# PSUM handed out in pairs of banks: one read for seven zones, for two heads' scores and for both row sums; maxima once per group; first loads in another order

## The chip, the cores and the metric

The kernel runs on one core of one Trainium2 chip, in float32. The metric is the device time of one execution in microseconds. The kernel before took 2783.18 us (median of 3 executions, 2778.69 to 2783.46). PE is TensorE, PEld its loading of weights, DVE VectorE, ACT ScalarE, POOL GpSimd, SP the engine that issues most of the transfers. PSUM holds what matmuls write: eight banks of 512 floats for each of 128 partitions.

## The reference

One layer of attention over graphs, with a layer norm before it. x is 128 graphs of 128 nodes by 768 features; adj is 128 x 128 for each graph; 12 heads of 64.

```python
h = jnp.maximum(_layernorm(x, axis=-1), 0.0)
q, k, v = (_split_heads(h @ W + b) for W, b in ((Wq, bq), (Wk, bk), (Wv, bv)))
scores = jnp.einsum('bhqd,bhkd->bhqk', q, k) / jnp.sqrt(HD)
scores = scores + beta * adj_e                       # adj_e = adj[:, None]
scores = jnp.where(adj_e > 0, scores, -9e15)
probs = jax.nn.softmax(scores, axis=-1)
out = x + merge_heads(jnp.einsum('bhqk,bhkd->bhqd', probs, v))
```

## The kernel before

The function `direct` does the work. It caps scores instead of subtracting their maximum; it keeps the largest row sums, reciprocals and biases that it sees in a small tile `seen`, and a second, general version would run if one of them passed a bound.

**Groups and slices.** The 128 graphs go in 32 groups of four, so that one matmul operand has 512 columns (4 graphs x 128 nodes). A group's projections are made in three slices: `qk0` (queries and keys of heads 0 to 5), `v`, and `qk1` (queries and keys of heads 6 to 11). Each slice multiplies a 2 x 3 by a 3 x 3 block matrix with 15 products in place of 18 (`PRODUCTS`), whose operands are sums of blocks: `SUMS_A` and `inner` make those of the activations (DVE at L411, POOL at L418 to L421), `SUMS_B` those of the weights. Products accumulate in four chains, a, b, c and d: the products of one chain add up in the same PSUM bank, and after each product the bank's running sum is read and added to, or subtracted from, the outputs that it belongs to.

**Two forms of a product.** Slices `qk0` and `v` of groups 1 to 31 use `product_z`, which splits a product once more, into seven zones of 128 columns (28 matmuls at L495). The prepared weights `T` of each product lie in DRAM and are loaded ahead by SP through a ring of five. A chain there holds two banks, zones 0 to 3 and 4 to 6. Slice `qk1` uses `product` (16 matmuls at L571 into one bank). After a product, the first read of an output ("opening") is made by ACT with the bias (L514 to L517 for qk0, L581 for qk1; in `v` half on DVE at L508 and L510), the others by DVE as an addition (L521 and L522 for the two banks of zones, L587 in qk1).

**Order.** `run` goes through the 15 slots of a slice. In a slot it issues the product's matmuls, then the steps written for that slot in `todo`, then the weighing of finished attention (`weighing`), then what is due from earlier slots (`later`), then the product's reads, then the "post" steps. From L981 to L1074 every engine's instructions stand in the order in which they are written; the start (group 0's first slice) and the last slice are ordered by a scheduler. The products of `product_z` come in the order `ZORDER`, chains by slot c, d, c, d, a, c, a, b, a, b, a, c, b, c, b. In qk1 the chains by slot are c, a, c, b, d, a, c, b, d, c, a, b, c, a, b.

**Attention.** `scores` makes the scores of two heads (one 128-feature block `oc`) for four graphs, one bank for each head (L609); DVE caps them and adds the bias (L613), ACT exponentiates (L616). `attend` gives eight steps of matmuls (L646) that `turn` puts one by one between the zones or columns of a slot's product; each of its two banks (r = 0 and 1) holds 4 x 65 columns, the 65th being the row sums. `weigh` bounds the sums (L623), takes reciprocals (L624), folds both into `seen` (L626), and then ACT divides, one activation for each graph and head (L630). POOL adds the block to x (L656), and SP stores it six slots later. In `qk0` of group G the attention of blocks 3 to 5 of group G-1 begins at slots `AV_Z`; in `qk1` that of blocks 0 to 2 of group G at slots `AV_AT`. The bias tile of the next group is made in `qk0` in steps (L436 to L449): a transpose, the mask, a masked copy on DVE (L444), a square on ACT (L445), a maximum into `seen`.

**Banks.** Eight bank tiles go round in a queue: `take` gives the one that has been free longest, `give` puts one back when its last reader has been issued.

```python
free = deque(psum.tile([P, W], F32, name=f"bank{i}") for i in range(8))
take, give = free.popleft, free.append
```

**Start.** Group 0 is made by `plain_slice` (L784) with unsplit products, beside the loading of the weights and the making of `T`; `raw_qk` and `raw_v` load the weights, `rows_1` and `rows_2` normalise the first x.

Of the kernel before, what the change touches and what calls it, by code (L numbers as in the profile page):

```python
# [17 lines left out]
P = 128  # L18
# [84 lines left out]
AV_Z = (7, 9, 12)  # L103
# [11 lines left out]
def direct(ctx, tc, x, adj, wq, bq, wk, bk, wv, bv, beta, out, bad):  # L115
# [31 lines left out]
    free = deque(psum.tile([P, W], F32, name=f"bank{i}") for i in range(8))  # L147
    take, give = free.popleft, free.append
# [31 lines left out]
    seen = const.tile([P, 20], F32, name="seen")  # L180

    over = const.tile([P, 44], F32, name="over")
# [19 lines left out]
    def raw_qk(u, t, parts):  # L202

        v = t.rearrange("p (c i j n) -> p c i j n", c=NC, i=2, j=3)
        for lo, hi in parts:
            for i, name in enumerate(("q", "k")):
                load_cols(nc.sync, v[:, :, i, lo:hi].rearrange("p c j n -> p c (j n)"), name, (lo + 3 * u) * P)
# [91 lines left out]
    raw_qk(0, flat(0, 9), ((0, 1),))  # L299
    load_x(0, 1)  # L300
    raw_qk(0, flat(0, 9), ((1, 3),))
# [131 lines left out]
    def bias_steps(G):  # L433
# [48 lines left out]
    def product_z(G, sl, n):  # L482
# [4 lines left out]
        if first:  # L487
            banks[chain] = (take(), take())
        p = [b.rearrange("p (z w) -> p z w", w=P) for b in banks[chain]]
        a, s, b = A[G, an], SP[G, n], tz.pop((G, sl, n))  # L490
        acts = (a[:, 0, 0:N], s[:, 1], s[:, 2], a[:, 1, 0:N], s[:, 3], a[:, 1, N:H2], s[:, 0])
        for z in range(7):
            lhs, rhs = (acts[z], b[:, z]) if sl == "v" else (b[:, z], acts[z])
            for q in range(0, P, HD):
                nc.tensor.matmul(p[z // 4][q:q + HD, z % 4, :], lhs[:, q:q + HD], rhs, start=(first and z % 4 == 0),  # L495
                                 stop=True, skip_group_check=True)
            turn()
        load_T()
        yield
        for (r, j), sign in uses:  # L500
            key = (G, sl, r, j)
            op = ALU.add if sign > 0 else ALU.subtract
            if key not in qk:
                left[key] = sum(k == (r, j) for q in PRODUCTS for k, _ in q[3])
                t = qk[key] = home_qk(*key, zones=True)
                if sl == "v":
                    bias = bv_b[:, j * 2 * P:(j + 1) * 2 * P]
                    added[G] = nc.vector.tensor_tensor(t[:, 0], bias[:, 0:P], p[0][:, 0], op)  # L508
                    nc.scalar.activation(t[:, 1:4], p[0][:, 1:4], AF.Copy, scale=float(sign))
                    added[G] = nc.vector.tensor_tensor(t[:, 6], bias[:, P:2 * P], p[1][:, 2], op)  # L510
                    nc.scalar.activation(t[:, 4:6], p[1][:, 0:2], AF.Copy, scale=float(sign))
                else:
                    oc = j + 3 * int(sl[2])
                    nc.scalar.activation(t[:, 0], p[0][:, 0], AF.Identity, bias=bqk[:, 0, oc:oc + 1], scale=float(sign))  # L514
                    nc.scalar.activation(t[:, 1:4], p[0][:, 1:4], AF.Copy, scale=float(sign))
                    nc.scalar.activation(t[:, 4:6], p[1][:, 0:2], AF.Copy, scale=float(sign))
                    opened[0] = nc.scalar.activation(t[:, 6], p[1][:, 2], AF.Identity, bias=bqk[:, 2, oc:oc + 1],  # L517
                                                     scale=float(sign))
            else:
                t = qk[key]  # L520
                nc.vector.tensor_tensor(t[:, 0:4], t[:, 0:4], p[0], op)  # L521
                added[G] = nc.vector.tensor_tensor(t[:, 4:7], t[:, 4:7], p[1][:, 0:3], op)  # L522
# [3 lines left out]
        if n == mine[-1]:  # L526
            for b in banks.pop(chain):
                give(b)
# [70 lines left out]
    def scores(G, u, order=(2, 0, 1)):  # L599

        order = [3 * u + j for j in order]
        ps = {(oc, i): take() for oc in order for i in range(2)}
        for oc in order:
            for g in range(GRP):
                keys, queries = (side(G, u, g // 2, oc % 3, i, g % 2) for i in (1, 0))
                for i in range(2):
                    r = slice(i * HD, (i + 1) * HD)
                    for k in range(0, N, HD):
                        nc.tensor.matmul(ps[oc, i][k:k + HD, g * N:(g + 1) * N], keys[r, k:k + HD], queries[r],  # L609
                                         start=True, stop=True)  # L610
# [7 lines left out]
    watched, recip = {}, {}  # L618

    def weigh(G, oc, r, pa, o):  # L620

        t = stat.tile([P, 2, 4], F32, tag="sm", name=f"sm_{G}_{oc}_{r}")
# [14 lines left out]
    def attend_steps(G, oc):  # L637
        o = work.tile([P, 2, 4, HD], F32, tag="o", name=f"o_{G}_{oc}", bufs=2)
        for r in range(2):
            bank = take()  # L640
            pa = bank[:, 0:4 * VE].rearrange("p (b e) -> p b e", e=VE)
            for g in range(2):
                for i in range(2):
# [5 lines left out]
                    if g == i == 1:  # L649
                        weighing.append(lambda r=r, pa=pa, bank=bank: (weigh(G, oc, r, pa, o[:, r])(), give(bank)))  # L650
# [14 lines left out]
    def scores_half(G, oc, r):  # L665
# [13 lines left out]
        e = es[G, oc, r] = work.tile([P, 2, 2, N], F32, tag="e", name=f"e_{G}_{oc}_{r}", bufs=6)  # L679
# [7 lines left out]
    def attend_half(G, oc, r):  # L687
# [15 lines left out]
        if not r:  # L703
            weigh(G, oc, r, pa, o)()
# [5 lines left out]
        at = 20 + 8 * (oc - 3)  # L710
        nc.vector.tensor_scalar(over[:, at:at + 4], pa[:, :, HD], SUM_CAP, None, op0=ALU.is_ge)
        nc.vector.tensor_scalar(over[:, at + 4:at + 8], pa[:, :, HD], 1.0 / SUM_CAP, None, op0=ALU.is_le)
        m = stat.tile([P, 2, 4], F32, tag="sm", name=f"sm_{G}_{oc}_{r}")
# [102 lines left out]

    turned[0, "raw"] = load_adj(0)
    nc.sync.dma_start(bv_b, bv[None, :].to_broadcast([P, D]))
    raw_v()
# [24 lines left out]
    def rows_2(g, mv, r):  # L844

        v = xg[0, g].rearrange("p b (c j) -> p c b j", c=NC)
        for k in range(3):
            n = work.tile([P, 2, P], F32, tag="e", name=f"rows_{g}_{k}", bufs=6)
# [149 lines left out]
    attention(0, 0, (11, 13, 15))  # L998
    for n in range(8):
        then(n, step, 2)  # L1000
# [87 lines left out]
    with tc.issue_after(watched[0].ins), tc.issue_after(recip[0].ins):  # L1088
        recip[0] = nc.vector.tensor_scalar(over[:, 0:20], seen, SUM_CAP, None, op0=ALU.is_ge)
# [4 lines left out]
    nc.tensor.matmul(pf[0:1, 0:44], ones, over, start=True, stop=True)  # L1094
    behind_recip(stores.pop(0), lambda: nc.vector.tensor_reduce(bad, pf[0:1, 0:44], AX.X, ALU.max))
# [129 lines left out]
```

## Time and profile before

| | |
|---|---|
| median of 3 executions | 2783.18 us (2778.69 to 2783.46) |
| the profiled execution | 2781.26 us, span 2779.2 us |
| TensorE clock granted over the span | 0.996 |
| PE busy | 2744.4 us, 99% |
| DVE, ACT, POOL busy | 2187.9 (79%), 1363.2 (49%), 2297.7 (83%) us |
| transfers | 660.87 MB, 238 GB/s over the span |

The time is that of the whole execution; the span is the part between the first and the last recorded instruction. A line of a group of instructions gives source line, engine, operation, output and inputs, shapes and count, then busy time in us, mean ns of one, and the idle time of the engine just before them with what ended it. A timeline line gives start and duration in us. A line of a stretch gives its length, then the busy time of PE, PEld, DVE, ACT and POOL with their counts, then the granted TensorE clock, the DMA share and GB/s.

### The profile page before, as it was taken

The numbers are of one execution on the slowest core, as the hardware profiler recorded it, in microseconds if no ns is written. First come the engines' busy times: TensorE is split into PE (matmuls) and PEld (weight loads), VectorE is DVE, ScalarE is ACT, GpSimd is POOL, SyncE is SP. The second block draws the span as 40 slices with busy tenths as digits, with TensorE's granted clock in tenths as the row PEclk, the third lists the DMA queues.
The fourth block names the chain that finished last, engine by engine and source line by source line (L and its number), as shares of the span: only waits on it lengthen the run. The fifth ranks groups of instructions, "written<-read, shape, count | busy, mean of one in ns | idle before, by whom it ended". The sixth has DMA issues, their size and how long they took to land.

```text
span 2779.2 us, 113442 instructions
## 1 busy us (share of the span) xinstructions
PE 2744.4 (99%) x46433; PEld 2401.3 (86%) x46433; DVE 2187.9 (79%) x4826; ACT 1363.2 (49%) x3999; POOL 2297.7 (83%) x4054
## 2 busy tenths in 40 slices
PE   8989999999999999999999999999999999999998
PEld 7678888899889998888989888988889989889887
DVE  5788878788878787787888787888787877878865
ACT  2445454555454554444554545554545544445543
POOL 3688988888988889888889888889888898888893
PEclk9999999999999999999999999999999999999999
DMA  8878878887878788778888788878787887788854
GB/s 212 232 239 235 237 236 236 267 251 230 239 228 258 253 249 237 234 232 264 255 238 233 233 239 268 255 228 242 226 261 253 249 234 237 231 265 253 232 185 129
DMA packets 526216, 660.87 MB, mean 238 GB/s; under 512 B 105460, under 2 KB 401664, under 8 KB 525696
## 3 DMA queue, kind: packets, MB, share of 16 engines
q1 hardware_dynamic: 525368, 653.20, 78.5%
q8 instruction: 368, 6.03, 0.9%
q14 instruction: 152, 1.25, 0.1%
q10 hardware_dynamic: 328, 0.40, 0.1%
HBM read 589.26 MB, written 64.21 MB: 235 GB/s over the span
## 4 chain that ended last, share of the span: by engine, by line


## 5 line engine op out<-in xcount | busy, mean ns | idle before, releaser
L630 ACT ACTIVATE o<-bank,sm 128x64 f32<-128x64 f32 x1524 | 354.7, 316 | 656.7 <-DVE sm L624 464.8
L495 PE MATMUL bank<-spbuf,T_qk 128*64 128x128 f32 x7440 | 660.6, 273 | 1.3 <-POOL spbuf L419 1.2
L495 PE MATMUL bank<-T_v,spbuf 128*64 128x128 f32 x7440 | 647.2, 273 | 0.1
L646 PEld LDWEIGHTS bank<-v,e 128*64 128x64 f32 x6048 | 419.3, 137 | 106.0 <-issue 0.8
L495 PEld LDWEIGHTS bank<-T_v,spbuf 128*64 128x64 f32 x7440 | 459.0, 137 | 0.4 <-ACT o L630 0.4
L495 PEld LDWEIGHTS bank<-spbuf,T_qk 128*64 128x64 f32 x7440 | 441.1, 137 | 2.1 <-POOL spbuf L419 1.4
L646 PE MATMUL bank<-v,e 128*64 128x65 f32 x6048 | 438.2, 221 | 0.2 <-ACT o L630 0.2
L495 PE MATMUL bank<-S,T_qk 128*64 128x128 f32 x4092 | 402.7, 274 | 2.5 <-DMA T_qk<-kept_qk 1.0
L495 PE MATMUL bank<-T_v,S 128*64 128x128 f32 x4092 | 402.0, 274 | 1.7 <-DVE v L521 0.7
L571 PE MATMUL bank<-S,wqk 128*64 128x256 f32 x2976 | 389.7, 380 | 0.0
L581 ACT ACTIVATE qk<-bank,bqk 128x256 f32<-128x256 f32 x372 | 156.6, 475 | 470.5 <-PE bank L571 362.2
L613 DVE SCALAR_TENSOR_TENSOR e<-bank,biasT 128x512 f32<-128x512 f32 x378 | 240.3, 685 | 90.4 <-PE bank L609 90.1
L571 PE MATMUL bank<-S,qk_T 128*64 128x256 f32 x2480 | 305.9, 379 | 0.0
L656 POOL TENSOR_TENSOR xo<-xo,o 128x512 f32<-128x512 f32 x189 | 242.4, 1283 | 50.0 <-ACT o L630 50.0
L551 POOL TENSOR_TENSOR v<-v 128x128 f32<-128x128 f32 x186 | 97.9, 526 | 224.5 <-DVE v L521 224.5
L495 PEld LDWEIGHTS bank<-T_v,S 128*64 128x64 f32 x4092 | 259.8, 137 | 8.8 <-issue 6.1
L521 DVE TENSOR_TENSOR v<-v,bank 128x512 f32<-128x512 f32 x310 | 211.7, 683 | 70.2 <-PE bank L495 60.5
L521 DVE TENSOR_TENSOR qk<-qk,bank 128x512 f32<-128x512 f32 x310 | 210.5, 679 | 68.0 <-PE bank L495 32.7
L495 PEld LDWEIGHTS bank<-S,T_qk 128*64 128x64 f32 x4092 | 249.1, 137 | 12.6 <-issue 4.6
L587 DVE TENSOR_TENSOR qk<-qk,bank 128x512 f32<-128x512 f32 (+1 forms) x311 | 207.8, 669 | 41.8 <-PE bank L571 31.5
L616 ACT ACTIVATE e<-e 128x512 f32<-128x512 f32 x378 | 230.7, 630 | 19.7 <-DVE e L613 17.9
L571 PEld LDWEIGHTS bank<-S,qk_T 128*64 128x64 f32 x2480 | 167.9, 137 | 58.9 <-issue 0.2
(164 smaller groups left out, 5923.3 us busy)
## 6 DMA issues: line engine op xcount, KB each, us to landing
T_qk<-kept_qk SPq DMA_DIRECT2D x465, 448.0 KB, 5.1
T_v<-kept_v SPq DMA_DIRECT2D x465, 448.0 KB, 4.8
x<-in_x_dram SPq DMA_DIRECT2D x254, 192.0 KB, 4.7
xo<-in_x_dram SPq DMA_DIRECT2D x189, 256.0 KB, 5.2
out_dram<-xo SPq DMA_DIRECT2D x189, 256.0 KB, 5.0
half<-in_x_dram SPq DMA_DIRECT2D x232, 192.0 KB, 3.8
adj<-in_adj_dram SPq DMA_DIRECT2D x128, 64.0 KB, 2.5
kept_qk<-prep_qk SPq DMA_DIRECT2D x15, 448.0 KB, 3.0
```

The costliest lines, as they stand in the source:

```text
L495: nc.tensor.matmul(p[z // 4][q:q + HD, z % 4, :], lhs[:, q:q + HD], rhs, start=(first and z % 4 == 0), stop=True, skip_group_check=True)
L521: nc.vector.tensor_tensor(t[:, 0:4], t[:, 0:4], p[0], op)
L551: e.tensor_tensor(v[:, 0:2, 0:HD], heads(0), heads(3), ALU.add)
L571: nc.tensor.matmul(p[q:q + HD, i, :], lhs[:, q:q + HD], rhs, start=(first and i == 0 and c == 0), stop=(c == 1), skip_group_check=True)
L581: opened[0] = nc.scalar.activation(t[:, i, :], p[:, i, :], AF.Identity, bias=bqk[:, i, oc:oc + 1], scale=float(sign))
L587: added[G] = nc.vector.tensor_tensor(t[:, :, cols], t[:, :, cols], p[:, :, cols], ALU.add if sign > 0 else ALU.subtract)
L613: taken[0] = nc.vector.scalar_tensor_tensor(e, ps[oc, i].rearrange("p (g n) -> p g n", g=GRP), SCORE_CAP * ISCALE, biasT[G], op0=ALU.min, ...
L616: nc.scalar.activation(e, e, AF.Exp, scale=1.0 / ISCALE)
L630: nc.scalar.activation(o[:, b], pa[:, b, 0:HD], AF.Copy, scale=t[:, 1, b:b + 1])
L646: nc.tensor.matmul(pa[q:q + HD, 2 * g + i, :], es[G, oc, i][:, 2 * r + g, q:q + HD], vt[G, "v", r, h // 4][:, 4 * g + h % 4, :], start=Tru ...
L656: nc.gpsimd.tensor_add(t, t, o.rearrange("p a (b j) d -> p (a b) (j d)", j=2))
```

## The change

- PSUM is cut into four tiles of two banks, `pairs`. `take2` and `give2` hand out whole pairs; `take` and `give` hand out halves of a pair, both halves of one pair being given out before another is opened.
- A chain of `product_z` holds a pair. Its seven zones are read by one DVE operation of 896 columns in place of two of 512 and 384; the opening read of qk0 is three ACT operations (128, 640, 128) in place of four, that of v one on DVE (zones 0 and 6 together) and one on ACT (640) in place of two and two.
- `scores` puts a block's two heads in a pair and reads them by one DVE operation and one exponential of 1024 columns in place of two of 512 each. The tiles `e` hold both heads, three of them in place of six.
- `attend` holds a pair for both r, and both are weighed together at its end: one bound, one reciprocal, eight divisions in a row. The row sums and reciprocals of a group are kept, and their maximum is taken once a group; `seen` has a column for each.
- `AV_Z` goes from (7, 9, 12) to (4, 8, 11).
- First loads: the first two column parts of q and k come before x, q's issued by SP and k's by ACT; the third part comes behind x rows 2 and 3; the weights of v and its bias come before adj.
- In groups 0 and 1 some steps move by two or three slots, and the tiles of the first rows become one tile for each graph.
- `product` and its lines stay as they are.

```diff
-AV_Z = (7, 9, 12)
+AV_Z = (4, 8, 11)
...
-    free = deque(psum.tile([P, W], F32, name=f"bank{i}") for i in range(8))
-    take, give = free.popleft, free.append
+    pairs = deque(psum.tile([P, 2, W], F32, name=f"pair{i}") for i in range(4))
+    halves_of, spare = {}, deque()
+
+    def take():
+        if not spare:
+            pair = pairs.popleft()
+            for h in range(2):
+                bank = pair[:, h]
+                halves_of[id(bank)] = (bank, pair, h)
+                spare.append(bank)
+        return spare.popleft()
+
+    def give(bank):
+        pair = halves_of[id(bank)][1]
+        for other in spare:
+            if halves_of[id(other)][1] is pair:
+                spare.remove(other)
+                pairs.append(pair)
+                return
+        spare.append(bank)
+
+    take2, give2 = pairs.popleft, pairs.append
...
-    raw_qk(0, flat(0, 9), ((0, 1),))
+    raw_qk(0, flat(0, 9), ((0, 1), (1, 2)), (nc.sync, nc.scalar))
     load_x(0, 1)
-    raw_qk(0, flat(0, 9), ((1, 3),))
+    raw_qk(0, flat(0, 9), ((2, 3),))
...
-        bm = stat.tile([P, GRP], F32, tag="bm", name=f"bm_{G}", bufs=1)
-        nc.vector.tensor_reduce(bm, a, AX.X, ALU.max)
-        nc.vector.tensor_tensor(seen[:, 16:20], seen[:, 16:20], bm, ALU.max)
+        nc.vector.tensor_reduce(seen[:, NG + G:NG + G + 1], a.rearrange("p g n -> p (g n)"), AX.X, ALU.max)
...
-            banks[chain] = (take(), take())
-        p = [b.rearrange("p (z w) -> p z w", w=P) for b in banks[chain]]
+            banks[chain] = take2()
+        p = banks[chain].rearrange("p i (z w) -> p (i z) w", w=P)
...
-                    nc.scalar.activation(t[:, 1:4], p[0][:, 1:4], AF.Copy, scale=float(sign))
-                    nc.scalar.activation(t[:, 4:6], p[1][:, 0:2], AF.Copy, scale=float(sign))
+                    nc.scalar.activation(t[:, 1:6], p[:, 1:6], AF.Copy, scale=float(sign))
...
-                nc.vector.tensor_tensor(t[:, 0:4], t[:, 0:4], p[0], op)
-                added[G] = nc.vector.tensor_tensor(t[:, 4:7], t[:, 4:7], p[1][:, 0:3], op)
+                added[G] = nc.vector.tensor_tensor(t, t, p[:, 0:7], op)
...
-        ps = {(oc, i): take() for oc in order for i in range(2)}
+        ps = {oc: take2() for oc in order}
...
+            e = work.tile([P, 2, W], F32, tag="e", name=f"e_{G}_{oc}", bufs=3)
             for i in range(2):
-                e = es[G, oc, i] = work.tile([P, GRP, N], F32, tag="e", name=f"e_{G}_{oc}_{i}", bufs=6)
-                taken[0] = nc.vector.scalar_tensor_tensor(e, ps[oc, i].rearrange("p (g n) -> p g n", g=GRP), SCORE_CAP * ISCALE,
-                                                          biasT[G], op0=ALU.min, op1=ALU.add)
-                give(ps[oc, i])
-                nc.scalar.activation(e, e, AF.Exp, scale=1.0 / ISCALE)
+                es[G, oc, i] = e[:, i].rearrange("p (g n) -> p g n", g=GRP)
+            bias = biasT[G].rearrange("p g n -> p (g n)")[:, None].to_broadcast([P, 2, W])
+            taken[0] = nc.vector.scalar_tensor_tensor(e, ps[oc], SCORE_CAP * ISCALE, bias, op0=ALU.min, op1=ALU.add)
+            give2(ps[oc])
+            nc.scalar.activation(e, e, AF.Exp, scale=1.0 / ISCALE)
...
-        nc.vector.tensor_scalar(t[:, 0], pa[:, :, HD], TINY, None, op0=ALU.max)
-        nc.vector.reciprocal(t[:, 1], t[:, 0])
-        s = seen[:, 8 * r:8 * r + 8]
-        watched[0] = nc.vector.tensor_tensor(s, s, t.rearrange("p i b -> p (i b)"), ALU.max)
+        n = pa.shape[1]
+        if G not in sums:
+            sums[G] = stat.tile([P, 6, 2, 2, 4], F32, tag="sm", name=f"sm_{G}", bufs=2)
+            weighed[G] = 0
+        t = sums[G][:, oc]
+        nc.vector.tensor_scalar(t[:, 0, 0:n], pa[:, :, :, HD], TINY, None, op0=ALU.max)
+        nc.vector.reciprocal(t[:, 1, 0:n], t[:, 0, 0:n])
+        weighed[G] += 1
+        if weighed[G] == 6:
...
+            watched[0] = nc.vector.tensor_reduce(seen[:, G:G + 1], sums[G][:, 0:3 if last else 6].rearrange(
+                "p o i r b -> p (o i r b)"), AX.X, ALU.max)
...
         def divide():
-            for b in range(4):
-                nc.scalar.activation(o[:, b], pa[:, b, 0:HD], AF.Copy, scale=t[:, 1, b:b + 1])
+            for r in range(n):
+                for b in range(4):
+                    nc.scalar.activation(o[:, r, b], pa[:, r, b, 0:HD], AF.Copy, scale=t[:, 1, r, b:b + 1])
...
+        pair = take2()
         for r in range(2):
-            bank = take()
-            pa = bank[:, 0:4 * VE].rearrange("p (b e) -> p b e", e=VE)
+            pa = pair[:, r, 0:4 * VE].rearrange("p (b e) -> p b e", e=VE)
...
-                    if g == i == 1:
-                        weighing.append(lambda r=r, pa=pa, bank=bank: (weigh(G, oc, r, pa, o[:, r])(), give(bank)))
+                    if r == g == i == 1:
+                        both = pair[:, :, 0:4 * VE].rearrange("p r (b e) -> p r b e", e=VE)
+                        weighing.append(lambda: (weigh(G, oc, both, o)(), give2(pair)))
...
+    raw_v()
+    nc.sync.dma_start(bv_b, bv[None, :].to_broadcast([P, D]))
     turned[0, "raw"] = load_adj(0)
-    nc.sync.dma_start(bv_b, bv[None, :].to_broadcast([P, D]))
-    raw_v()
...
-        then(13 + g, norm, 1, g)
+        if g < 3:
+            then(15 + g, norm, 1, g)
...
-    then(9, lambda: mom.extend(moments_1(1, 0, GRP * NB)))
-    then(11, lambda: moments_2(1, 0, GRP * NB, *mom))
+    then(12, lambda: mom.extend(moments_1(1, 0, GRP * NB)))
+    then(14, lambda: moments_2(1, 0, GRP * NB, *mom))
     for n in range(18):
-        then(n, step, 1 + (n % 3 == 1))
+        then(n, step, 1 + n % 2)
...
+    then(0, norm, 1, 3)
     for n in range(8):
-        then(n, step, 2)
+        then(2 + n, step, 2)
```

More of the change, by code (lines that the diff above doesn't have):

```diff
@@ L177, in direct @@
     nc.gpsimd.memset(ones, 1.0)
-    seen = const.tile([P, 20], F32, name="seen")
-    over = const.tile([P, 44], F32, name="over")
+    NS = 2 * NG + 1
+    seen = const.tile([P, NS], F32, name="seen")
+    over = const.tile([P, NS + 24], F32, name="over")
     nc.gpsimd.memset(seen, 0.0)
@@ L494, in product_z @@
             for q in range(0, P, HD):
-                nc.tensor.matmul(p[z // 4][q:q + HD, z % 4, :], lhs[:, q:q + HD], rhs, start=(first and z % 4 == 0),
+                nc.tensor.matmul(p[q:q + HD, z, :], lhs[:, q:q + HD], rhs, start=(first and z % 4 == 0),
                                  stop=True, skip_group_check=True)
@@ L526, in product_z @@
         if n == mine[-1]:
-            for b in banks.pop(chain):
-                give(b)
+            give2(banks.pop(chain))
         yield
@@ L847, in rows_2 @@
         for k in range(3):
-            n = work.tile([P, 2, P], F32, tag="e", name=f"rows_{g}_{k}", bufs=6)
+            if not k:
+                first["rows", g] = work.tile([P, 3, 2, P], F32, tag="e", name=f"rows_{g}", bufs=3)
+            n = first["rows", g][:, k]
             first["dve"] = nc.vector.tensor_scalar(n.rearrange("p c (b j) -> p c b j", b=NB), v[:, 2 * k:2 * k + 2], mv[:, 0:1], r, op0=ALU.subtract,
@@ L1093, in direct @@
     pf = take()
-    nc.tensor.matmul(pf[0:1, 0:44], ones, over, start=True, stop=True)
-    behind_recip(stores.pop(0), lambda: nc.vector.tensor_reduce(bad, pf[0:1, 0:44], AX.X, ALU.max))
+    nc.tensor.matmul(pf[0:1, 0:NS + 24], ones, over, start=True, stop=True)
+    behind_recip(stores.pop(0), lambda: nc.vector.tensor_reduce(bad, pf[0:1, 0:NS + 24], AX.X, ALU.max))
 @with_exitstack
```

38 lines of the change are left out of this document (20 added, 18 removed).

## The prediction

> **What bounds the kernel now.** I read the page's first part, then the busy time by stretches, then one group slice by slice, then PE's waits, then the order of single instructions. Page:
>
> ```profile
> span 2779.2 us, 113442 instructions
> PE 2744.4 (99%) x46433; PEld 2401.3 (86%) x46433; DVE 2187.9 (79%) x4826; ACT 1363.2 (49%) x3999; POOL 2297.7 (83%) x4054
> ```
>
> PE is the bound; 35 us of the span are not PE. The stretches (length, busy time of PE, PEld, DVE, ACT, POOL, then PE's clock) say where:
>
> ```profile
> 0.00:30.00 30.00, 21.82 (x122) 19.04 (x123) 13.21 (x41) 8.55 (x22) 5.68 (x23) 0.94 0.91 180
> ...
> 200.00:2700.00 2500.00, 2497.63 (x43271) 2192.94 (x43266) 2001.54 (x4362) 1262.83 (x3703) 2148.26 (x3799) 1.00 0.80 242
> 2700.00:2780.00 80.00, 70.82 (x1184) 59.94 (x1181) 44.41 (x131) 29.25 (x95) 34.90 (x59) 0.97 0.45 143
> ```
>
> From 200 to 2700 us PE idles 2.4 us in 2500: DVE, ACT or POOL time saved there buys nothing, while every wait put before a matmul is paid whole. The slices of group 10 (qk0, v, qk1):
>
> ```profile
> 904.22:933.38 29.16, 29.16 (x614) 28.28 (x612) 23.92 (x50) 16.90 (x54) 27.83 (x49) 1.00 0.80 256
> 933.38:960.28 26.90, 26.70 (x520) 25.43 (x518) 22.02 (x47) 15.89 (x38) 18.60 (x34) 1.00 0.85 281
> 960.28:988.90 28.62, 28.62 (x340) 20.02 (x338) 21.97 (x54) 9.86 (x34) 26.14 (x47) 1.00 0.76 195
> ```
>
> A group is 84.7 us. PE's waits by releaser (total us, times, longest) are few, nearly all from the start:
>
> ```profile
> PE bank L784 <- DMA spbuf<-in_L_gnn_Wk_dram: 4.7, 2, 3.2
> PE bank L495 <- DVE v L521: 4.1, 3, 3.5
> ```
>
> The qk1 slice, slot 1 of group 10:
>
> ```profile
> 962.01 1.90 PE L571 MATMUL bank<-A,wqk 128*64 128x256 f32 x16
> ...
> 962.23 0.84 ACT L581 ACTIVATE qk<-bank,bqk 128x256 f32<-128x256 f32 x2 [10.09 <-PE bank L571]
> ...
> 967.51 0.69 DVE L587 TENSOR_TENSOR qk<-qk,bank 128x512 f32<-128x512 f32 x1 [0.19 <-PE bank L571]
> ```
>
> Slot 1's matmuls start at 962.01, and ACT begins to read slot 0's bank 0.22 later, for 0.84. Reading the last product lies beside the matmuls of the next, because these write another bank tile. A DVE read is 0.69.
>
> **Part 1, halves of a pair in the qk1 slice (`product`): the large term.** Its text is untouched, but take() now hands out halves of four pair tiles. Chain c (slot 0) and chain a (slot 1) get the two halves of one pair, b (slot 3) and d (slot 4) those of another. By slot the chains are c a c b d a c b d c a b c a b. In the changed program's instruction list the first matmul of a product waits for the read of the product before wherever both lie in one pair: slots 1, 2, 4, 6, 8, 10 and 13, in every group from 1 to 30. In the list of before no such matmul waits on a read nearer than 20 matmuls. So the overlap just shown is gone seven times a group:
> - Slots 1, 2, 6 (ACT reads, two of 256): 0.22 until the read starts by the lines above, 0.84 for it, 0.05 from a read's end to a matmul's start (the matmul of L495 at 1464.99 behind the read of L521), 0.05 because the first eight matmuls after such a stall take 487 ns where 437 is usual: 1.16 us each.
> - Slots 4, 10 (one DVE read of 512): 0.22 + 0.69 + 0.10 = 1.01.
> - Slot 8: the same, behind one attention step's maximum and reciprocal (rows of 155 and 178 ns): 1.34.
> - Slot 13: the same, behind a sum (0.8 to 0.96 us) and row statistics in DVE's queue. Bounds 1.01 (queue empty, since DVE gains time by the earlier stalls) and 2.0; I take 1.3.
>
> Sum 3 x 1.16 + 2 x 1.01 + 1.34 + 1.30 = 8.14 us a group, x30 = **244 us**. Bounds: all DVE reads at 1.01, 7.5 a group, 226; every DVE read behind a 0.9 us sum as well, 11.1, 334. I take the low side: those sums are issued in a slot's beginning and end before its last matmul.
>
> At this place the trace can be weighed against a rule. The Trainium skill, "PSUM — Partial Sum Buffer", "Summary: rules for kernel authors", says to let a read that runs beside matmuls target another bank and to guard by bank. By that rule these seven waits are needless, since a half is a bank of its own; the lines above agree (two banks, both engines at once), and the sum would be without the 244, the rival of 2846 below. The program's list has them all the same, and a wait in it is obeyed.
>
> **Part 2, attention moved in the z slices (7,9,12 to 4,8,11).** Attention from slot 4 is weighed in slot 6 of qk0. ACT's queue there is the bias square, then eight divides in a row, then the opening reads of slot 6's product (chain a), which slot 8 writes again. Before, ACT at that place:
>
> ```profile
> 918.33 0.63 ACT L445 ACTIVATE adjT<-adjT 128x512 f32<-128x512 f32 x1 [0.81 <-DVE biasT L444]
> 918.87 0.35 ACT L514 ACTIVATE qk<-bank,bqk 128x128 f32<-128x128 f32 x1
> 919.12 0.48 ACT L515 ACTIVATE qk<-bank 128x384 f32<-128x384 f32 x1
> 919.49 0.39 ACT L516 ACTIVATE qk<-bank 128x256 f32<-128x256 f32 x1
> 919.75 0.38 ACT L517 ACTIVATE qk<-bank,bqk 128x128 f32<-128x128 f32 x1
> ```
>
> The square waits for the bias's chain on DVE (L439 to L444, 2.3 us, behind slot 4's reads), starts about 1.56 us into slot 6 and holds ACT 0.54. Four divides in a row take 0.93 (L630 at 921.76; 0.20 each after the first), so eight hold ACT 1.62, until 3.72. From start to start the reads above take 0.25, 0.37 for 384 and 0.26 for 256 (0.86 ns an element), so the new three of 128, 640 and 128 take 0.25 + 0.59 + 0.38, until 4.95; PE at 5.05. A z slot is 1.53 here and each attention step adds 0.115, so slot 8 would start at 1.64 + 1.53 = 3.17: stall 1.88. Before, this read ended 0.4 us into slot 8 and its second bank was wanted only at 0.9. x29 groups = **54.5 us**, plus 1.3 in group 1 and 0.7 in group 31. Bounds: 0 (the bias chain runs 1.9 us earlier) and 2.3 (DVE's half-wide row up). I take 1.88, as that chain's order on DVE is as before.
>
> **Part 3, one read for seven zones.** 620 DVE reads of 896 for pairs of 512 and 384. By slope (683 - 551 ns over 128 elements) the 896 is near 1.08 us; it must end before the same chain's next product one slot (1.53 us) on: 0.22 + 1.08 + 0.05 = 1.35, with 0.1 to 0.2 left. DVE saves about 65 ns of issue each, 40 us, hidden behind PE. Cost 0; bounds 0 and, at 0.1 for about 10 handovers a group, 30.
>
> **Part 4, scores, row sums, maxima.** 189 merged score reads (1024 wide, about 1.2 us against 0.685 twice) and 189 merged exponentials (1.07 against 0.63 twice); 381 small maxima (366 ns) become about 32. That frees some 12 + 130 us of DVE, all beside PE: 0. The score pair comes free 0.5 us later for its first half, wanted slots later: 0. The divides, eight at once, are ACT's 49%; the one place where they are in the way is part 2. The xo add on POOL (1.28 us) starts after all eight, and its store is six slots behind: 0.
>
> **Part 5, the start.** Raw parts of q and k go on two queues, part (2,3) behind x rows 2 and 3, adj behind v; norms and moments move two or three slots, onto a next slice's slot 0 for the fourth. The two waits on Wk (4.7 us) may shrink, by SP issuing half as much; but the DMA share is 0.91 over these 30 us, so bytes limit, and the moments' banks share a pair with products there (2 to 3 stalls of 1 us). I take 0; bounds -10 (both waits on Wk, the wait of 3.5 on DVE, and 1.6 of halved clock behind one of them, see below) and +6 (three such stalls and x 3 us later, hidden by half).
>
> **Part 6, the rest.** In the last group a scheduler weaves the same pairs: five stalls, +5 (0 to 10); v slice of group 1: +3 (0 to 4).
>
> **Sum.** 244 + 54.5 + 1.3 + 0.7 + 0 + 0 + 0 + 5 + 3 = 309. The profiled run took 2781.3 (span 2779.2), so 3090; it stands 1.9 below the median of 2783.2, which changes nothing here.
>
> **The rivals.**
> - *The clock drops too.* After PE idles of about 3 us the clock halves in this trace, for 1.6 us lost each time (length, PE busy, ..., clock):
>
> ```profile
> 24.35 9.98 PE L784 MATMUL bank<-A,spbuf 128*128 128x256 f32 x38 [3.21 <-DMA spbuf<-in_L_gnn_Wk_dram]
> ...
> 24.35:28.00 3.65, 3.65 (x10) 2.97 (x11) 2.69 (x5) 1.51 (x6) 0.00 (x0) 0.57 0.83 205
> 28.00:32.00 4.00, 4.00 (x20) 3.52 (x19) 4.00 (x9) 0.84 (x2) 2.98 (x4) 1.00 1.07 213
> ```
>
>   Idles of 1.0 to 1.5 us did not do it (11 to 14 us: clock 1.00). The new idles are 1.0 to 1.9 but repeated. Once a group: 3090 + 30 x 1.6 = 3138; three times: 3234. The Trainium skill, "TensorE: Matmul & The Clock Gate", "A second HAM failure mode: psum-queue depth-cycling", tells of just such frequent micro-idles making the clock swing; no run here shows it yet. Chance 0.10.
> - *Half the stalls are short.* ACT's late read in slot 8 doesn't bite, as the bias chain gains from the qk1 stalls: 3090 - 56 = 3034. Chance 0.12.
> - *The half-pair waits cost nothing*, the reads being done when they are reached: 3090 - 244 = 2846. Against it: the reads can't start before their product's last matmul. Chance 0.03.
> - *Faster: the first loads decide.* Place: the first 100 us; price: up to -10, 2771 to 2779. It decides only if each of the 210 handovers costs under 0.05 us and the read in slot 8 is early as well. For it: 35 us of PE idle lie at the ends. Chance 0.02.
>
> **How the numbers follow.** The likeliest case, 0.73, is 3090, its own range 3050 to 3150 (226 to 290 for part 1, 30 to 67 for part 2). The range takes in 3034 and the clock once a group: 3030 to 3165, some 0.15 left out. About 0.2% (5.6 us) is what a measurement of this kernel can tell from no change: faster 0.02, same 0.01, slower 0.97.
>
> **What the changed profile would show.** Right: PE's share near 89%; at the head of PE's waits the `product` matmul on the ACT read, about 90 times and 100 us, and on the DVE read, about 120 times and 130 us; the z matmul on ACT's last opening read, about 29 times and 54 us; the qk1 slice at 36.8 us, qk0 at 31, v at 26.9; clock 1.00. Wrong: qk1 near 28.6 us, or matmuls of 2x duration in clock windows under 1.0, or z slices with a wait at every DVE read (part 3's bound).

## The result and the profile after

The changed kernel took 3099.02 us (median of 6 executions, 3094.85 to 3100.24) against 2779.72 for the kernel before (6 executions, 2778.69 to 2783.46): 1.114 times as long, 95% interval 1.113 to 1.116. The forecast was 3090. The page of the kernel after:

```profile
span 3094.5 us, 109778 instructions
PE 2796.4 (90%) x46433; PEld 2386.1 (77%) x46433; DVE 1924.6 (62%) x3073; ACT 1285.2 (42%) x3438; POOL 2254.4 (73%) x4054
```

DVE has 263 us less to do and ACT 78, and the span is 315 us longer. PE issues the same 46433 matmuls. By stretches (length; busy time of PE, PEld, DVE, ACT, POOL; PE's clock, DMA share, GB/s):

```profile
60.00:100.00 40.00, 23.27 (x104) 19.49 (x103) 27.53 (x74) 3.42 (x13) 17.77 (x27) 0.79 0.71 220
...
250.00:3010.00 2760.00, 2519.64 (x43006) 2159.21 (x43002) 1733.22 (x2673) 1178.85 (x3141) 2082.81 (x3750) 1.00 0.73 217
```

The steady part, which had 2.4 us of idle PE in 2500 before, now has 240 us of it in 2760, at a clock of 1.00. The three slices of group 10, qk0, v and qk1:

```profile
1001.65:1032.61 30.96, 29.27 (x614) 28.24 (x612) 19.16 (x28) 16.48 (x51) 26.41 (x47) 1.00 0.78 242
1032.61:1059.15 26.54, 26.54 (x520) 25.42 (x518) 19.13 (x23) 14.26 (x26) 16.80 (x31) 1.00 0.85 283
1059.15:1095.98 36.83, 30.27 (x341) 20.11 (x338) 21.20 (x42) 9.46 (x33) 27.86 (x53) 1.00 0.59 151
```

Before they were 29.16, 26.90 and 28.62: qk0 is 1.8 us longer and qk1 8.2; v is 0.4 shorter in this group, but over groups 2 to 30 it takes 26.5 us in both kernels. PE's waits (by releaser: total us, times, longest):

```profile
PE pair L585 <- DVE qk L601: 108.6, 120, 1.1
PE pair L585 <- ACT qk L595: 88.2, 90, 1.0
PE pair L514 <- ACT qk L533: 52.0, 31, 2.2
PE pair L812 <- DVE mean L356: 16.3, 2, 15.9
```

The first two are the handovers between neighbours in one pair, 7 in each of 30 groups; the third is slot 8 of qk0; the fourth, in the start, was not foreseen. Here is slot 1 of the qk1 slice in the timeline (start, duration, in brackets the idle time before and what ended it):

```profile
1061.12 0.84 ACT L595 ACTIVATE qk<-pair,bqk 128x256 f32<-128x256 f32 x2 [9.34 <-PE pair L585]
...
1062.01 1.95 PE L585 MATMUL pair<-A,wqk 128*64 128x256 f32 x16 [0.93 <-ACT qk L595]
```

Before, slot 1's matmuls started 0.22 us ahead of ACT's read of slot 0; now they start when it has ended, 1061.12 + 0.84 + 0.05. And ACT's queue ahead of slot 8 of qk0:

```profile
1016.48 0.63 ACT L466 ACTIVATE adjT<-adjT 128x512 f32<-128x512 f32 x1 [0.28 <-DVE sm L642]
1017.02 1.73 ACT L655 ACTIVATE o<-pair,sm 128x64 f32<-128x64 f32 x8
1018.59 0.41 ACT L531 ACTIVATE qk<-pair,bqk 128x128 f32<-128x128 f32 x1
1018.84 0.76 ACT L532 ACTIVATE qk<-pair 128x640 f32<-128x640 f32 x1
1019.43 0.43 ACT L533 ACTIVATE qk<-pair,bqk 128x128 f32<-128x128 f32 x1
...
1019.91 0.44 PE L514 MATMUL pair<-S,T_qk 128*64 128x128 f32 x4 [1.69 <-ACT qk L533]
```

Square, eight divisions, three opening reads, and PE 0.05 us behind the last: the queue is the one of the forecast, without a gap in it.

The whole difference of the spans, 315.3 us, can be laid out by the starts of each slice's first matmul in the two traces (means over groups 2 to 30):

| part | before | after | difference | forecast |
|---|---|---|---|---|
| qk1, groups 1 to 30 | 28.70 each | 36.80 | +243 | +244 |
| qk0, groups 2 to 30 | 29.21 | 30.96 | +50.8 | +54.5 |
| v, groups 2 to 30 | 26.54 | 26.50 | -1 | 0 |
| until group 1's first matmul | 128.7 | 139.0 | +10.3 | 0 (-10 to +6) |
| group 1, qk0 and v | 71.2 | 71.8 | +0.6 | +4.3 |
| group 31, qk0 and v | 57.6 | 61.6 | +4.0 | +0.7 |
| last qk1 to the end | 44.1 | 51.7 | +7.6 | +5 |

### The profile page after: what moved, and what is told of

Same layout as the page of the kernel before. It is cut to its first block, busy times and chain, and to the rows that moved or that the text cites. A ratio compares the mean times of both kernels' runs of the same rounds, so it can differ in the third digit from the quotient of the medians.

```text
span 3094.5 us, 109778 instructions
## 1 busy us (share of the span) xinstructions
PE 2796.4 (90%) x46433; PEld 2386.1 (77%) x46433; DVE 1924.6 (62%) x3073; ACT 1285.2 (42%) x3438; POOL 2254.4 (73%) x4054
## 4 chain that ended last, share of the span: by engine, by line
## 5 line engine op out<-in xcount | busy, mean ns | idle before, releaser
L514 PE MATMUL pair<-spbuf,T_qk 128*64 128x128 f32 x7440 | 654.9, 273 | 0.0
L514 PE MATMUL pair<-T_v,spbuf 128*64 128x128 f32 x7440 | 645.8, 273 | 0.0
L537 DVE TENSOR_TENSOR qk<-qk,pair 128x896 f32<-128x896 f32 x310 | 337.1, 1087 | 321.8 <-PE pair L514 267.4
L585 PE MATMUL pair<-S,wqk 128*64 128x256 f32 x2976 | 403.0, 384 | 106.6 <-DVE qk L601 76.6
L671 PEld LDWEIGHTS pair<-v,e 128*64 128x64 f32 x6048 | 407.8, 137 | 112.1
L514 PEld LDWEIGHTS pair<-T_v,spbuf 128*64 128x64 f32 x7440 | 456.4, 137 | 0.0
L514 PE MATMUL pair<-S,T_qk 128*64 128x128 f32 x4092 | 400.9, 274 | 53.4 <-ACT qk L533 52.0
L514 PEld LDWEIGHTS pair<-spbuf,T_qk 128*64 128x64 f32 x7440 | 434.2, 137 | 0.0
L671 PE MATMUL pair<-v,e 128*64 128x65 f32 x6048 | 433.5, 222 | 0.0
L514 PE MATMUL pair<-T_v,S 128*64 128x128 f32 x4092 | 401.1, 274 | 5.9 <-DMA T_v<-kept_v 2.5
L514 PEld LDWEIGHTS pair<-S,T_qk 128*64 128x64 f32 x4092 | 246.9, 137 | 70.8 <-ACT qk L533 59.5
L514 PEld LDWEIGHTS pair<-T_v,S 128*64 128x64 f32 x4092 | 256.4, 137 | 13.0 <-issue 5.3
```

The costliest lines, as they stand in the source:

```text
L514: nc.tensor.matmul(p[q:q + HD, z, :], lhs[:, q:q + HD], rhs, start=(first and z % 4 == 0), stop=True, skip_group_check=True)
L537: added[G] = nc.vector.tensor_tensor(t, t, p[:, 0:7], op)
L585: nc.tensor.matmul(p[q:q + HD, i, :], lhs[:, q:q + HD], rhs, start=(first and i == 0 and c == 0), stop=(c == 1), skip_group_check=True)
L671: nc.tensor.matmul(pa[q:q + HD, 2 * g + i, :], es[G, oc, i][:, 2 * r + g, q:q + HD], vt[G, "v", r, h // 4][:, 4 * g + h % 4, :], start=Tru ...
```

## The experiments

### Which chains share a pair

The first theory says that the loss in qk1 comes from neighbouring products in one pair, and from nothing else about the pairs. So the text of `product` was made to choose the partner. In the first kernel c and d share, and a and b:

```diff
+    mates, held = {'c': 'cd', 'd': 'cd', 'a': 'ab', 'b': 'ab'}, {}
...
-            banks[chain] = take()
+            if G < NG - 1:
+                mate = mates[chain]
+                if mate not in held:
+                    held[mate] = [take2(), len(mate)]
+                banks[chain] = held[mate][0][:, mate.index(chain)]
+            else:
+                banks[chain] = take()
```

> The changed kernel, but in the qk1 slices of groups 1 to 30 chains c and d share a pair and a and b another (before: c with a, b with d). Nothing else is changed. If the stalls come from neighbouring products in one pair: neighbours are then left at slots 9, 11 and 14 alone, all behind a DVE read, so 3 waits a group instead of 7, 90 in all on the DVE read and none on the ACT read, each about 1.0 us with the drain: qk1 slice 36.8 - 8.1 + 3.1 = 31.8 us, time 3099 - 150 = 2949 (2935 to 2965). If the rival holds, that reads of half a pair or the tiles as such are slow wherever the halves lie: no change, 3099, qk1 36.8.

Measured: 2977.05 us (1.070 of before, 1.069 to 1.072), 122 us less than the change, with qk1 at 32.9 us.

```profile
PE pair L593 <- DVE qk L609: 97.8, 90, 1.2
```

The list has 90 waits, as expected. The time is 28 us above the expectation and outside its range. By the lengths of the slots in the two traces (means over the 30 groups) the three handovers cost 1.29, 1.28 and 1.35 us, not 1.0. In slots 11 and 14 the DVE read stands behind an attention step's bound and reciprocal (1045.74 and 1053.20 in group 10), in slot 9 behind row statistics: the price of a DVE handover was too low for those places. The other 0.30 us of a group are a wait in slot 6 that is too short for the list, which leaves out idle times under 0.15 us:

```profile
1032.79 1.78 ACT L603 ACTIVATE qk<-pair,bqk 128x256 f32<-128x256 f32 x4 [3.38 <-DVE qk L609]
```

```profile
1031.72 1.90 PE L593 MATMUL pair<-S,qk_T 128*64 128x256 f32 x16
1033.68 0.65 PE L593 MATMUL pair<-S,wqk 128*64 128x256 f32 x4
```

The first two of these four activations (0.84 us) read slot 4's product (chain d), late, while PE is already in slot 5. Chain c in slot 6 lies in the other half of that pair and starts 0.05 us after they end. So two users of a pair that are two slots apart can still wait for each other, if the read between them is late.

In the second, a and b have a pair each, and c and d share with products 9 and 10 exchanged:

```diff
+QORDER = (0, 1, 2, 3, 4, 5, 6, 7, 8, 10, 9, 11, 12, 13, 14)
...
+    mates, held = {'c': 'cd', 'd': 'cd', 'a': 'a', 'b': 'b'}, {}
...
-        slice_of(G, "qk1", todo)
+        slice_of(G, "qk1", todo, QORDER)
```

> The changed kernel, but in qk1 of groups 1 to 30 chains a and b have a pair each (half of it unused), c and d share one, and products 9 and 10 change places, so that no product follows another in the same pair. Neighbour theory: no wait on an ACT or DVE read of the product before; qk1 28.7 to 29.1 us (attention, with one pair left, waits up to 0.2 us twice a group for the divisions before it); time 3099 - 231 to 243, 2856 to 2868. Rival (pairs cost in other ways in qk1, such as attention's divisions eight in a row): qk1 stays above 30.

Measured: 2891.13 us (1.040, 1.038 to 1.042), qk1 29.9. The list has no wait of `product` on a read any more, and the wait that the expectation has in brackets is there, twice a group, larger than expected:

```profile
PE pair L515 <- ACT qk L534: 51.5, 31, 2.2
...
PE pair L687 <- ACT o L671: 13.3, 60, 0.3
```

With one pair left for attention, its next matmuls wait for the eight divisions before: 13.3 us on record, and about 0.2 us more of lost time at each of the 60 stops, together 0.89 us a group. The short wait in slot 6 is the same as in the first kernel, since c and d still share: 0.30. Both make the 1.2 us by which qk1 is still longer than before.

So in the third the two pairs are taken in turn, which leaves two for attention: partners as in the first, order 1, 0, 3, 2, 5, 4, 7, 6, 10, 8, 11, 9, 13, 12, 14.

> The changed kernel, but in qk1 of groups 1 to 30 chains c and d share one pair, a and b another, and the products come as 1, 0, 3, 2, 5, 4, 7, 6, 10, 8, 11, 9, 13, 12, 14, so that the two pairs alternate; two pairs are left for attention. If the neighbours in one pair are all of the loss in qk1, and what qk1_apart kept (29.9 against 28.7 us) was attention waiting for its divisions with one pair: qk1 28.7 to 28.9, time 3099 - 240 = 2859 (2854 to 2866). If pairs cost something else in qk1: 29.5 or more, above 2880.

Measured: 2965.33 us (1.066, 1.065 to 1.068). The expectation fell by 106 us. The neighbours were apart, but two new waits a group had come, 93.2 us in 60:

```profile
1034.68 0.65 PE L594 MATMUL pair<-S,wqk 128*64 128x256 f32 x4 [1.44 <-ACT qk L604]
1040.66 0.65 PE L594 MATMUL pair<-A,wqk 128*64 128x256 f32 x4 [1.83 <-ACT qk L604]
```

The timeline of ACT and DVE ahead of them shows where they come from:

```profile
1033.79 0.84 ACT L604 ACTIVATE qk<-pair,bqk 128x256 f32<-128x256 f32 x2 [3.54 <-DVE qk L610]
1038.13 1.75 ACT L671 ACTIVATE o<-pair,sm 128x64 f32<-128x64 f32 x8 [3.50 <-DVE sm L659]
1039.71 0.89 ACT L604 ACTIVATE qk<-pair,bqk 128x256 f32<-128x256 f32 x2
```

```profile
1031.09 0.85 DVE L433 TENSOR_TENSOR S<-A,A 128x512 f32<-128x512 f32 x1 [3.00 <-PE pair L594]
1031.87 1.00 DVE L396 BATCH_NORM_STATS2 strow<-half 128x6 f32<-128x384 f32 x2
```

The new order had put a sum that overwrites an operand into the slot whose product still reads it, so that DVE waited 3.0 us, its read came late and ACT's at 1033.79 after it: the first wait. And it had put an opening read behind eight divisions on ACT (slot 7), as in qk0: the second. So the order is to blame; whether the alternation costs something by itself is for the next kernel. The fourth keeps the alternation and has every opening read before the divisions, and three sums (2, 3 and 5; the fourth stays in slot 6) and one transpose a slot later:

```diff
+QORDER = (1, 0, 5, 2, 10, 4, 3, 6, 7, 8, 11, 9, 13, 12, 14)
...
-        at_slots(to_hT, G, ((2, ("A10",)), (9, ("A12",))))
-        at_slots(sum_acts, G, ((2, (0,)), (3, (2,)), (5, (3,)), (6, (4,)), (7, (5,)), (10, (1,)), (11, (6,)), (12, (7,)),
+        at_slots(to_hT, G, ((2, ("A10",)), (10, ("A12",))))
+        at_slots(sum_acts, G, ((2, (0,)), (4, (2,)), (6, (3, 4)), (8, (5,)), (10, (1,)), (11, (6,)), (12, (7,)),
```

> As alternate (two pairs taken in turn by qk1's products), but in the order 1, 0, 5, 2, 10, 4, 3, 6, 7, 8, 11, 9, 13, 12, 14, so that every opening read on ACT comes before attention's divisions, and with four sums and one transpose of the next group a slot later, so that DVE doesn't wait for the slot's own matmuls. If what alternate lost (two waits of 1.4 and 1.8 us a group on ACT) came from that order, they go: qk1 28.7 us, 3099 - 243 = 2856 (2850 to 2866). If alternating pairs cost it: still above 2900.

Measured: 2853.82 us (1.026, 1.025 to 1.028), 245 us less than the change where the forecast put 244 on these handovers. qk1 takes 28.71 us, against 28.70 before. The first lines of PE's waits have no `product` any more:

```profile
PE pair L515 <- ACT qk L534: 51.0, 31, 1.7
PE pair L828 <- DVE mean L357: 16.1, 2, 15.7
PE pair L828 <- ACT A L905: 5.5, 1, 5.5
```

Pairs, merged reads, merged scores and merged divisions are all still there. That settles part 1: the same wide tiles cost nothing in qk1 when neighbours don't share one.

### The wait in slot 8 of qk0

Two kernels take away one part each of ACT's queue. The first moves attention off slot 4:

```diff
-AV_Z = (4, 8, 11)
+AV_Z = (5, 8, 11)
```

> The changed kernel with attention in qk0 and at the end of a group at slots 5, 8, 11 in place of 4, 8, 11: the eight divisions leave ACT's queue of slot 6. My theory (square, divisions, then the opening read that slot 8 waits for): the wait in slot 8 goes from 1.7 us to 0 to 0.1, qk0 30.96 to 29.3 us, time 3099 - 48 = 3051 (3046 to 3056). Rival (the wide opening read, 128 + 640 + 128 from one tile, is itself too slow for two slots): the wait stays above 1 us, time above 3080.

The second leaves attention and moves the masked copy and the square a slot back:

```diff
-            bias(G + 1, 3, 5, 6, 12)
+            bias(G + 1, 3, 5, 7, 12)
```

> The changed kernel with the masked copy and the bias square of qk0 in slot 7 in place of slot 6; the divisions stay in slot 6. By my theory the divisions then begin about 1.1 us into slot 6, the opening reads at 2.7, and they end at 4.0 where slot 8 would start at 3.2: the wait falls from 1.7 to about 0.85 us, qk0 30.1, time 3099 - 25 to 30 = 3070 to 3074. If the square alone were the cause, the wait would go: 3050. If it had no part: 3099.

Measured: 3071.39 us without the divisions (1.105, 1.103 to 1.107), 3069.48 with the later square (1.104, 1.102 to 1.106). In the second the wait was halved as worked out, and qk0 came to 30.04 us:

```profile
PE pair L514 <- ACT qk L533: 25.4, 31, 2.2
```

In the first the wait of L514 on ACT is gone, and qk0 is 29.3 as expected, but the time is 20 us above the expectation. It went to the next slice, v, 27.4 us in place of 26.5, where the score matmuls now wait for POOL:

```profile
PE pair L623 <- POOL qk L557: 11.0, 31, 0.4
PE pair L623 <- POOL qk L556: 7.7, 29, 1.6
```

POOL decodes the outputs of qk0 (L554 to L557), and it had 27.8 us of work in the 29.2 us of that slice before. With the stall in slot 8 gone it has 1.7 us less for it, and is late; what in its queue makes it so is tried further down.

### The start

PE's single long wait, 15.9 us at 90 us, is on the mean of the moments (L356). Is it a half-pair wait too? The bank of the moments was given a pair of its own, so that no product shares a tile with it:

```diff
-        bank = pm[G, lo, "bank"] = take()
+        pair = pm[G, lo, "bank"] = take2()
+        bank = pair[:, 0]
```

> The changed kernel, but the bank of the moments (L350) is a pair of its own, so no product shares a tile with it. Theory: the wait of 15.9 us at the matmul of L812 on the mean of L356 is again a half-pair wait; without it PE goes on with the next product into a free pair, and the time falls by 12 to 16 us: 3083 to 3087. Rival: DVE stood still for 8 us behind a store of prepared weights, and PE would soon have waited for DVE's read of its own product anyway: a wait of 8 us or more on L825 appears in its place, 3091 to 3099.

Measured: 3092.77 us, 6 less than the change. Neither theory has it right. The wait moves to the moments' own second matmul:

```profile
PE pair L368 <- DVE dev L361: 13.3, 2, 13.2
```

That is a true dependence, and both have their cause in DVE's queue, in the kernel after:

```profile
77.04 0.70 DVE L457 STREAM_TRANSPOSE adjT<-adj 128x512 f32<-128x512 f32 x1
85.72 0.29 DVE L272 TENSOR_TENSOR prep_v<-v_B 128x128 f32<-128x128 f32 x1 [7.98 <-DMA kept_v<-prep_v]
...
89.81 0.18 DVE L356 TENSOR_REDUCE mean<-pair 128x16 f32<-128x32 f32 x1
```

DVE stood 8 us behind a preparation step that waited for a store of prepared weights; the moments, moved from slot 9 to 12, had come to stand behind that step. The kernel before has such a stop too:

```profile
84.91 0.29 DVE L251 TENSOR_TENSOR prep_v<-spbuf 128x128 f32<-128x128 f32 x1 [6.97 <-DMA kept_qk<-prep_qk]
```

There the first half of the moments was done by 75.6 us and their bank was their own, so PE ran past that stop. The other test puts back the order of the first loads and all steps of groups 0 and 1:

```diff
-    raw_qk(0, flat(0, 9), ((0, 1), (1, 2)), (nc.sync, nc.scalar))
+    raw_qk(0, flat(0, 9), ((0, 1),))
...
-    then(12, lambda: mom.extend(moments_1(1, 0, GRP * NB)))
-    then(14, lambda: moments_2(1, 0, GRP * NB, *mom))
+    then(9, lambda: mom.extend(moments_1(1, 0, GRP * NB)))
+    then(11, lambda: moments_2(1, 0, GRP * NB, *mom))
```

> The changed kernel with the first loads and the steps of groups 0 and 1 (norms, moments, preparation) in the order of before; pairs as in the change. If the new order is what puts group 1's first matmul at 139.0 us (before 128.7): it comes at 129 to 132 and the time is 3089 to 3092. If the pairs are what does it (the moments' half): still 135 or later, above 3095.

Measured: 3092.40 us. Group 1's first matmul comes at 134.1, between the two: the order is worth 4.9 of the 10.3 us. In what is left stand half-pair waits of the moments:

```profile
PE pair L367 <- DVE v L825: 5.2, 1, 5.2
...
PE pair L353 <- DVE st L342: 3.4, 1, 3.4
PE pair L812 <- DVE mean L356: 3.4, 1, 3.4
```

The wait on L342 was there before as well; those on L825 and on the mean are between a product and the moments in one pair. The one on L825 is long because that read, too, stands behind a stop of DVE for a store (6.61 us, until 83.61). With the old order and a pair for the moments together, in the last two kernels below, group 1 starts at 132.6 and 131.0. PE's longest wait in their start is that of group 0's scores (7.6 and 6.3 us); what else is left against 128.7 is open.

### All mends together

If these causes are all, a kernel without them should be level with the kernel before, and any gain of the merged operations that the stalls had hidden would show.

> All mends together: alternating pairs in every qk1 slice, the last included (its order 1, 0, 3, 2, 5, 6, 7, 9, 10, 4, 11, 12, 13, 8, 14), the masked copy and square in slot 7, four of the eight divisions behind the slot's reads, the moments in a pair of their own. Expected: qk1 28.8, qk0 29.3, v 26.5, as before; start 4 us later to 4 earlier; the end 3 to 6 us longer: 2782 (2772 to 2795), that is level with the kernel before within 0.5%. If merged reads had a gain of their own that the stalls hid, it would be under 2770.

Beside the edits shown above, with the partners of the first pairing kernel:

```diff
-LAST = (0, 1, 2, 3, 5, 7, 6, 10, 11, 9, 4, 12, 8, 13, 14)
+LAST = (1, 0, 3, 2, 5, 6, 7, 9, 10, 4, 11, 12, 13, 8, 14)
...
+    def halve(divide, pair):
+        divide((0,))
+        rest.append(lambda: (divide((1,)), give2(pair)))
...
-                        weighing.append(lambda: (weigh(G, oc, both, o)(), give2(pair)))
+                        weighing.append(lambda: halve(weigh(G, oc, both, o), pair))
```

`halve` issues four of the eight divisions at once and the other four behind the slot's reads. Measured: 2911.35 us (1.047, 1.046 to 1.049), 129 us above the expectation, with the third experiment's order still in it (68.9 us of its two waits) and 32 us of waits on POOL's decoding. With the order of the fourth, the old start, and only block 5's divisions split (`if oc == 5` in the last line above):

> alternate2 in every group, and: masked copy and square in slot 7, half of the divisions of block 5 alone behind slot 6's reads, moments in a pair of their own, first loads and steps of groups 0 and 1 as before, last slice in the alternating order. Expected: qk0 29.1 (as in best2), v 26.5, qk1 28.7, a group 84.3 against 84.45; start: group 1 at 129 to 131 (before 128.7), with no wait of moments on a product's read; the end 0 to 4 us longer: 2780 (2772 to 2788). If merged reads bring anything by themselves, it is under 2772; if other false waits come up, above 2788.

Measured: 2827.18 us (1.017, 1.015 to 1.018), 47 us above the expectation. Groups lost 1.3 us each, in v, and nothing in qk0 and qk1. POOL and PE in group 10 of this kernel:

```profile
951.48 1.28 POOL L709 TENSOR_TENSOR xo<-xo,o 128x512 f32<-128x512 f32 x1
952.72 0.73 POOL L556 TENSOR_TENSOR qk<-qk 128x256 f32<-128x256 f32 x1
...
954.34 0.46 POOL L558 TENSOR_TENSOR qk<-qk 128x128 f32<-128x128 f32 x1
```

```profile
954.85 0.45 PE L640 MATMUL pair<-qk 64*64 64x128 f32 x8 [0.61 <-POOL qk L558]
```

POOL has no gap here; the third block's addition stands ahead of the fifth of six decodings, which the scores wait for (before, at 938.39, ahead of the sixth). The next kernel puts it behind:

```diff
-        later(add, 2)
+        later(add, 4 if oc == 4 else 2)
...
-    then((SC_AT, "post"), scores, 0, 0)
+    for n, j in ((4, 2), (5, 0), (6, 1)):
+        then((n, "post"), scores, 0, 0, (j,))
```

> best3 with two changes: POOL's xo addition of qk0's third block (block 4) comes two slots later, behind the decoding of qk0's last outputs; and group 0's scores come at slots 4, 5, 6 of its qk1 in place of all at slot 1. If best3's waits of the score matmuls on POOL's decoding (29.5 us and drains, about 1.4 us a group) came from that addition of 1.28 us ahead of the decoding: they go, and so does the wait of 7.6 us at 97.8: 2827 - 40 - 5 = 2782 (2775 to 2792). If POOL is behind in qk0 for another reason (it has 27.8 us of work in 29.2): part of them stays, 2800 or more.

Measured: 2789.41 us (1.0034, 1.0022 to 1.0046), inside the expectation. A group of this kernel, and the same of the kernel before:

```profile
904.74:989.34 84.60, 84.60 (x1468) 77.24 (x1465) 60.51 (x93) 40.26 (x109) 71.70 (x129) 1.00 0.80 243
```

```profile
904.22:988.98 84.76, 84.56 (x1466) 73.74 (x1464) 67.99 (x149) 42.73 (x126) 72.65 (x129) 1.00 0.80 243
```

PE is full in both, and 7.5 us less of DVE work in each group buys nothing: over groups 2 to 30 a group takes 84.57 us against 84.45. That is 3.5 of the 9.9 us between the two spans (2789.1 and 2779.2). Another 5.0 lie in qk0 and v of group 31, where PE waits 4.7 us for loads of T, and 1.3 at the end. The start is 2.3 us later, with a wait of 6.3 us on group 0's scores that the second edit moved but didn't remove, and group 1 gains as much back. No version tried is faster than the kernel before.

## Why the prediction was right, and where it was not

**Part 1** held in mechanism and size: 243 us against 244, undone by the fourth pairing kernel (245). By the lengths of the slots (means over the 30 groups, after less before) the handovers of ACT cost 1.16, 1.22 and 1.22 us in slots 1, 2 and 6, where 1.16 was forecast, and those of DVE 1.11 and 0.96 in slots 4 and 10 (1.01), 1.29 in slot 8 (1.34) and 1.14 in slot 13 (1.30, between 1.01 and 2.0): 8.10 against 8.14. The waits on record are shorter, 88.2 / 90 = 0.98 us for ACT and 108.6 / 120 = 0.91 for DVE, and so the forecast waits of 100 and 130 us in PE's list were too long. The difference, (243 - 196.8) / 210 = 0.22 us a handover, stands in the records as busy PE. That PE's pipeline runs empty at each stop would fit, but isn't shown, since the ends of matmuls are modelled in these records.

**Part 2** held: 1.75 us a group against 1.88, with the square and the divisions each shown to have their share (with the later square, a wait of 25.4 / 31 = 0.82 us where 0.85 was expected). What the forecast lacked was the cover underneath: with the stall taken away, POOL is next in line in qk0, 0.9 us a group, 26 us in all. Its sentence that the addition "starts after all eight" and costs nothing is right only while that stall gives POOL time.

**Parts 3 and 4** at nothing: right. The read of 896 took 1087 ns where 1.08 us was worked out, v stayed at 26.5, and DVE was freed of 263 us where the terms of these parts make 182; the last kernel shows that the freed time of DVE has no use with PE full.

**Part 5** was wrong, and outside its bounds: +10.3 us where 0 (-10 to +6) was said. The step that failed is "norms and moments move two or three slots": it was priced by the banks that they share, and the queue that they were moved past was left out. DVE's queue there holds preparation steps that wait for stores, one of them for 8 us, and PE waits for the moments behind it. It could be read in the trace of before, where DVE stands still for 6.97 us at that place. The half-pair waits ("2 to 3 stalls of 1 us") were mis-sized too: with the old order they are 5.2 and 3.4.

**Part 6**: the end cost 7.6 for 5; group 1 cost 0.6 for 4.3; three waits on T in the last group (3.1 us) weren't foreseen. These misses of both signs, the start's and part 2's add up to the 6 us by which the sum of 309 missed 315: that the sum came out closer than the start's term did is luck.

**The rivals.** The clock did not drop: 1.00 over 2760 us with all the new stops in it. The Trainium skill, "TensorE: Matmul & The Clock Gate", "A second HAM failure mode: psum-queue depth-cycling", has a clock that swings with frequent micro-idles; with idles of 0.7 to 1.7 us, eight in a group, this trace doesn't show it. The read in slot 8 of qk0 did bite (52.0 us), the half-pair waits were not free, and the start did not gain. The Trainium skill, "PSUM — Partial Sum Buffer", "Summary: rules for kernel authors", would guard by bank; the waits measured here are by tile. No run let a matmul write one half of a pair while another engine read the other, so whether the chip would have allowed it isn't shown, only that the program never did it.

## What to carry to other kernels

In this program the unit of a dependence in PSUM was the tile as it was allocated, not the bank or the slice: a pool that hands out halves of a larger tile turns the neighbours in it into a chain, also in code whose text is untouched. Before a buffer is widened, list which users follow each other in time and keep those in different tiles. With the users alternating, and no read late, the same wide tiles cost nothing. Before a step is moved, look at what stands in the queue that it is moved past. And a merged operation only pays on the engine that bounds: here it freed 263 us of an engine that wasn't, and made one queue (eight divisions in a row) long enough to stand ahead of a read that was.

## What the runs showed of the hardware beyond that

A stop of PE can cost more than its recorded wait: 0.22 us more at each handover in qk1 (243 us lost, 196.8 recorded, 210 stops), but only 0.07 in slot 8 of qk0 (1.75 lost, 52.0 / 31 = 1.68 recorded).

From 250 to 3010 us the granted clock stayed at 1.00 with idles of up to 1.7 us, eight in each group. In the kernel before, an idle of 3.21 us halved it (0.57 from 24.35). But in the start of the kernel after, the clock was at half behind an idle of 1.98 us, which ended at 174.87, and at 1.00 behind one of 2.19 us, which ended at 159.25:

```profile
160.00:164.00 4.00, 4.00 (x94) 4.00 (x90) 2.87 (x6) 0.00 (x0) 3.77 (x6) 1.00 0.80 115
176.00:179.40 3.40, 3.40 (x36) 3.40 (x34) 0.42 (x1) 1.58 (x3) 3.32 (x4) 0.50 0.44 77
```

So the length of one idle doesn't settle it in these traces; what does is open.
